# First eight microseconds of a residual-fusion kernel: one weight split moved to VectorE, tile 1 gathered in three parts and transposed between the first products

## The chip, the cores and the metric

The kernel runs on one core of a Trainium2 chip. The metric is the device time of one execution in microseconds (us), less is better. Three runs of the kernel before gave 101.44, 101.99 and 107.20 us; the median is 101.99 us.

## The reference

`x` has 4 rows of 1024 x 512, `cond` is 4 x 256, `W` is 1536 x 512, `b` has 512 numbers, all in 32-bit floats.

```python
hidden = concatenate([cond, cond], axis=-1)                  # 4 x 512
x_mean = mean(x, axis=1, keepdims=True)
fused  = concatenate([x, x_mean * ones, hidden * ones], -1)  # 4 x 1024 x 1536
return x + relu(einsum('bld,do->blo', fused, W) + b)
```

The first third of `W` multiplies `x` itself (4096 x 512 by 512 x 512, nearly all of the arithmetic). The second third multiplies the row's mean and the last third the condition; both, with `b`, are one bias vector for each of the 4 rows, which is added before the relu.

## The kernel before

The 4096 lines of `x` are 32 tiles of 128 x 512. For a product on TensorE a tile has to be transposed in four chunks of 128 columns, `j` from 0 to 3. For accuracy each operand is split into a high part in the reduced type `F32R` and a low part, which is what the high part leaves over, and a tile's result is the sum of 12 matrix products: for each chunk high x high (`n` = 0), low x high (`n` = 1) and high x low of `W` (`n` = 2). So there are 384 products of 128 x 512, on five PSUM banks `ps_o` (`po` in the profile); two more banks `ps_x` (`px`) and one `acc` take transposed chunks.

Every instruction stands in a table `ORDER`, written out by hand (lines 22 to 50). An engine runs its own instructions in that order and waits for what each of them reads, or for a buffer to be free. A name in the table is a task, and `@d`, `@a`, `@p` put it on VectorE (DVE), ScalarE (ACT) or GpSimd (POOL):

- `W0` to `W3` and `X0.0` to `X0.3` load the four chunks of `W`'s first third and the tiles 0 to 3; `Z4.1` and the like load later tiles in a layout that VectorE transposes.
- `y1.0` gathers part 0 of tile 1 (line 239 on DVE and POOL, 237 on ACT): it copies columns so that TensorE can transpose a chunk. `Y_PARTS` tells how many chunks a part has.
- `T1.0` transposes chunk 0 of tile 1 on TensorE (line 259) into a bank; the line above it says which.
- `h1.0` makes the high part on ACT (line 268, two instructions, the second reads the column sums), `l1.0` the low part on DVE (line 274).
- `wh1` makes the high part of chunk 1 of `W` (lines 218 and 220), `wl1` its low part (line 224). `wh0l` and `wh0r` are the left and right half of 256 columns.
- `p0.2.1` is the product of tile 0, chunk 2, `n` = 1 (line 365). A `fill` (line 134) is a product of zeros that keeps TensorE at work until data are there.

The tiles 0 to 3 go this way, one after the other; from tile 4 on, VectorE does the transposes. At the start the first tile's products are held up by what they need, chunk by chunk: the four chunks of `W` come in at some distance, `wl1` and `wl2` are made by POOL, `wh2` and `wh3` by ACT, and ACT also makes every `h`. In the table before, tile 1's two parts are gathered by `y1.0@d` and `y1.1@a`, its four transposes stand together behind `p0.0.1` and go to `acc`, `ps_o[3]`, `ps_x[0]` and `ps_x[1]`, and chunk 0 of `W` gets its low part from POOL.

Of the kernel before, what the change touches and what calls it, by code (L numbers as in the profile page):

```python
# [20 lines left out]

ORDER = """
W0@a fill X0.0 X0.1 W1 fill relu fill W2 fill X0.2 fill W3 fill X0.3 Z4.1 y0.0@d y0.1@a y0.2@p fill T0.0 T0.1 h0.0
T0.2 T0.3 fill wh0r@d h0.1 wh0l@d p0.0.0 wl0r@p l0.0@d h0.2 wl0l@p y1.0@d y1.1@a p0.0.1 h0.3 l0.1@d T1.0 T1.1 T1.2
T1.3 wh1@d h1.0 p0.0.2 l1.0@d h1.1 p0.1.0 p1.0.0 Z4.2 h1.2 p0.1.1 l0.2@d l0.3@d wl1@p p1.0.2 l1.1@d h1.3 p1.0.1 Z4.3
p1.1.0 wh2@a l1.2@d p1.1.1 y2.0@d p0.2.0 wl2@p l1.3@d T2.0 T2.1 T2.2 T2.3 p1.2.0 Z4.0 p0.2.1 h2.0 h2.1 h2.2 h2.3
l2.0@d l2.1@d wh3@a C p1.2.1 p0.1.2 p1.1.2 l2.2@d l2.3@d wl3@d p2.0.0 p2.0.1 p0.2.2 V p0.3.0 B p1.3.0 y3.0@d p0.3.1
p1.3.1 T3.0 T3.1 T3.2 T3.3 p1.2.2 p0.3.2 h3.0 h3.1 p1.3.2 l3.0@d h3.2 l3.1@d p2.0.2 h3.3 l3.2@d l3.3@d p2.1 p2.2 p2.3
p3.0 p3.1 Z5.0 Z5.2 Z5.3 p3.2 Z5.1 T4.0 T4.3 h4.0 T4.1 h4.3 l4.0@d h4.1 l4.3@p t3 p3.3 T4.2 M1 K2@d l4.1@p M0 K1@a
p4.0 t2 M2 h4.2 ac0@p p6.0 M3 l4.2@d K0@a p4.3 Z6.2 t0 K3@d p5.3 t1 Z6.3 ac1@d g0.0 p7.2 p6.2 d0.0 Z6.0 g0.1 p5.2 d0.1  # L30
g1.0 p5.0 Z6.1 T5.1 T5.3 p5.1 d1.0 T5.2 p6.3 K5@a Z7.0 T5.0 as0 p4.2 to0 g1.1 p7.3 Z7.3 h5.1 m0.0 p6.1 g2.0 l5.1@p
m0.1 p4.1 Z7.2 h5.2 m0.2 p7.1 K4@a m0.3 h5.3 p7.0 Z7.1 K6@a p8.1 l5.3@p l5.2@d h5.0 X4.1 p10.1 f0 Z8.2 d1.1 p9.1 fa0
Z8.1 p10.3 l5.0@d vh0 d2.0 p8.2 g2.1 vl0 Z8.0 p11.2 K7@a T6.3 d2.1 p11.3 T6.2 h6.3 Z8.3 p8.0 T6.0 l6.3@p T6.1 pb0
p10.0 bc0@a h6.0 p10.2 b1@p h6.1 X1.1 l6.0@d p9.3 X2.0 h6.2 b2@d p9.0 as1 Z9.2 to1 p9.2 r1@a l6.1@p l6.2@d p12.3 r2@a
X1.0 m1.0 K9@a p8.3 Z9.0 F1@p T7.3 p11.0 T7.1 h7.3 p12.2 b0@p m1.1 h7.1 p12.0 T7.2 K8@a p12.1 b3@p g3.0 T7.0 p11.1
K10@a m1.2 Z10.3 h7.2 d3.0 p13.1 Z9.3 m1.3 h7.0 p14.0 Z9.1 l7.0@d f1 b4@p p13.3 r0@a l7.2@d p14.1 r3@a T8.2 l7.3@p
p15.0 fa1 Z10.2 p13.0 T8.0 vh1 F2@p p15.1 K11@a vl1 X5.0 p13.2 F0@d Z10.0 b6@p p15.2 S1 T8.3 pb1 X5.1 l7.1@p p14.3
bc1@a as2 p14.2 K13 F3@p r6@a p16.0 K12 h8.3 p15.3 K14 h8.2 l8.3@p T8.1 p17.0 b5@d h8.1 p19.3 b9@p h8.0 p17.3 r4@a
l8.0@d p19.2 to2 g3.1 l8.2@d F4@p p16.2 r5@a m2.0 p18.3 K15 b8@p S4 p18.2 Z10.1 m2.1 p16.3 X3.1 d3.1 m2.2 p19.0 m2.3
p18.1 F5@p T9.0 p16.1 f2 fa2 p20.3 b11@p S5 T9.3 S2 p17.2 vh2 X3.0 h9.0 vl2 p17.1 F6@p X2.1 h9.3 S3 T9.2 p19.1 l8.1@d  # L40
b7@p S6 p20.0 X4.0 pb2 S0 p18.0 bc2@a l9.3@p X7.0 h9.2 p20.2 K17 r7@a p20.1 K16 as3 F7@p p22.2 T9.1 l9.0@d p21.3 h9.1
T10.0 S7 r8@a p21.1 l9.1@p X6.1 K19 r11@a p22.1 r9@a l9.2@d b10@p p22.0 r14@a K18 p21.2 r13@a T10.1 h10.0 p24.2 F13@p
T10.2 h10.1 p24.1 T10.3 h10.2 F8@p F9@d p21.0 r15@a p24.0 r10@a F11@p S8 K20 h10.3 p22.3 S13 K21 r17@a p23.1 X6.0 to3
r21@a p23.0 F10@p m3.0 r18@a p23.3 r20@a m3.1 p26.1 l10.3@p m3.2 p25.0 K22 F21@p p23.2 m3.3 r22@a p26.2 F15@p f3 S21
p24.3 S11 r12@a fa3 p27.3 S10 F17@p K23 S15 vh3 p25.1 S9 r16@a vl3 p25.2 r19@a F16@p r23@a p26.0 l10.0@d p25.3 F19@p
S16 pb3 X7.1 p26.3 bc3@a S17 F12@p P28 p27.1 K25 p27.2 l10.2@d P30 F18@p p28.2 F14@d r25@a p30.2 l10.1@p K26 p28.0 S14
S18 F25@d P31l p27.0 S19 F23@p r26@a p30.0 K24 S25 p31.2l F26@p S23 K27 p31.0l r24@a S12 p31.1l P29 p31.3l F20@p p30.3
P31r F31l F22@d S31l p29.1 S26 p28.1 S20 r27@d S22 p29.0 F24@d F27@p p28.3 p29.3 F28 S24 p30.1 S27 S28 p29.2 F30
p31.1r F29 S30 p31.0r p31.3r S29 p31.2r F31r S31r
""".split()  # L50


# [1 line left out]
def kernel(  # L54
# [9 lines left out]
    B, L, D = x.shape  # L64
# [9 lines left out]
    E = 4  # L74
    UNITS = [(0, 1), (1, 1), (2, 1), (3, 1)] + [(t, 4) for t in range(4, NT, 4)]
    BY_PE = (0, 1, 2, 3)
    Y_PARTS = {0: [(0, 1), (1, 1), (2, 2)], 1: [(0, 2), (2, 2)]}
    X_SLOT = [2, 3, 4, 5, 0, 1, 2, 3]
    X_PARTS = {0: [(0, 1), (1, 1), (2, 1), (3, 1)]}
    W_SLOT, COND_SLOT = 0, 1  # L80
# [34 lines left out]
    ps_o = [banks.tile([P, D], F32, name=f"po{i}") for i in range(O_BANKS)]  # L115
    ps_x = [banks.tile([P, D], F32, name=f"px{i}") for i in range(2)]
    acc = banks.tile([P, D], F32, name="acc")
# [23 lines left out]
    def task(name):  # L141
        def put(f):
            assert name not in tasks, name
            tasks[name] = f
        return put
# [17 lines left out]
    def z_of(u):  # L163
        return (u - len(BY_PE)) % Z_BUFS

    @task("relu")
    def _(e):
        nc.scalar.activation(one, one, AF.Relu)
# [58 lines left out]
    def gathered(t):  # L227
        return parks[PARKS - 1 - t]

    for t in range(sum(UNITS[u][1] for u in BY_PE)):  # L230
        for h, (j0, n) in enumerate(Y_PARTS.get(t, [(0, J)])):
            @task(f"y{t}.{h}")
# [8 lines left out]
    for u, (t0, n) in enumerate(UNITS):  # L241
        r = t0 // NK
        s = row_units[r].index(u)
        for j in range(J):
            buf, col = place[u, j]
            m = n * P
            if u == 0:
                xT = ((ps_x[0], ps_x[1], ps_o[4], ps_o[4])[j])[:, j % 2 * m : (j % 2 + 1) * m]
            elif u in BY_PE:
                xT = (ps_o[4] if u == 3 and j == 1 else (acc, ps_o[3], ps_x[0], ps_x[1])[j])[:, :m]  # L250
            else:
                xT = (turned if j % 2 else ps_x)[j // 2]

            @task(f"T{u}.{j}")
            def _(e, u=u, j=j, t0=t0, n=n, xT=xT):
                if u in BY_PE:
                    for i in range(n):
                        v = gathered(t0 + i)[:, j * P : (j + 1) * P]
                        nc.tensor.transpose(xT[:, i * P : (i + 1) * P], v, ident)  # L259
                    return  # L260
                nc.vector.transpose(  # L261
                    xT.rearrange("p (n q e) -> p n q e", q=Q // E, e=E),
                    zs[z_of(u)][:, : n * NQ].rearrange("p n (q j e) -> p n j q e", j=J, e=E)[:, :, j],
                )

            @task(f"h{u}.{j}")
            def _(e, r=r, j=j, s=s, xT=xT, buf=buf, col=col, m=m):
                nc.scalar.activation(  # L268
                    his[buf][:, col : col + m], xT, AF.Copy, accum_out=sums[:, r, j, s : s + 1]
                )  # L270

            @task(f"l{u}.{j}")
            def _(e, xT=xT, buf=buf, col=col, m=m):
                nc_of[e].tensor_tensor(  # L274
                    los[buf][:, col : col + m], xT, his[buf][:, col : col + m].bitcast(F32), ALU.subtract
                )
# [114 lines left out]
    for t in range(NT):  # L391
        r, k = divmod(t, NK)
        if t == LAST:
            for h in range(2):
                d = slice(h * HALF, (h + 1) * HALF)
# [93 lines left out]
```

## Time and profile before

| | us |
|---|---|
| median of the 3 runs | 101.99 |
| lowest and highest run | 101.44, 107.20 |
| the profiled execution | 101.22 |
| its span, from the first instruction to the last | 99.4 |
| TensorE (PE) busy in the span | 94.5 |
| GpSimd (POOL) busy | 79.6 |
| VectorE (DVE) busy | 77.5 |
| ScalarE (ACT) busy | 61.6 |

The profile is of one execution of its own, whose time was 101.22 us: 1.8 us lie around the span. Moments in the rows count from the span's start. A matmul overlaps the next one, so that its own duration is longer than its share of the time; the chain of waits gives each only what it adds.

### The profile page before, as it was taken

Reading aid. Unit: us, or ns where it says so; the run is one execution under the profiler, and the core shown is the slowest. Engines: PE = TensorE matmul, PEld = TensorE weight load, DVE = VectorE, ACT = ScalarE, POOL = GpSimd, SP = SyncE. Lnnn points to the kernel's source line nnn. Section 1 sums busy time; section 2 is a strip of 40 time slices with the busy share of each in tenths; the row PEclk is TensorE's granted clock in tenths of the full one; section 3 lists DMA queues with packets and bytes.
Section 4 is the critical chain, followed back from the end, with each engine's and each line's share of the span. In section 5 each row is a group of like instructions: output and inputs, shape, how many; then the busy total and the mean of one; then the engine's idle time right before and its main releaser. Section 6 shows DMA issues by size and latency. Waiting matters only on the chain.

```text
span 99.4 us, 1448 instructions
## 1 busy us (share of the span) xinstructions
PE 94.5 (95%) x424; PEld 76.4 (77%) x424; DVE 77.5 (78%) x132; ACT 61.6 (62%) x160; POOL 79.6 (80%) x77
## 2 busy tenths in 40 slices
PE   6999999999999999999999999999999999999940
PEld 2468888888888888888888888888888887888830
DVE  1396559959498979989699899899769769969930
ACT  4495338555996699994299227499973897350000
POOL 5287002969869989999999999999999999999600
PEclk9999999999999999999999999999999999999999
DMA  2999999999999999999999999999998369998894
GB/s 49 343 346 283 213 301 287 204 263 330 198 209 209 222 250 216 234 345 241 219 215 226 246 374 291 381 297 407 407 391 263 115 255 304 331 382 329 303 381 151
DMA packets 25361, 27.36 MB, mean 275 GB/s; under 512 B 1413, under 2 KB 16009, under 8 KB 25354
## 3 DMA queue, kind: packets, MB, share of 16 engines
q1 hardware_dynamic: 25210, 27.01, 101.0%
q10 hardware_dynamic: 144, 0.26, 0.8%
q8 instruction: 3, 0.05, 0.2%
q14 instruction: 4, 0.03, 0.1%
HBM read 18.88 MB, written 8.39 MB: 274 GB/s over the span
## 4 chain that ended last, share of the span: by engine, by line
PE 95%; DVE 1%; issue 0%
PE po L365 88%; PE po L134 4%; PE px L259 1%; PE acc L343 1%; PE po L259 1%; PE acc L259 0%; DVE x L403 0%; DVE warm L125 0%; DVE one L126 0%
## 5 line engine op out<-in xcount | busy, mean ns | idle before, releaser
L365 PE MATMUL po<-w_hi,hi 128*128 128x512 f32 (+1 forms) x132 | 50.5, 385 | 0.0
L365 PE MATMUL po<-w_hi,lo 128*128 128x512 f32 (+1 forms) x132 | 50.3, 384 | 0.0
L365 PE MATMUL po<-w_lo,hi 128*128 128x512 f32 (+1 forms) x132 | 50.1, 384 | 0.0
L454 POOL TENSOR_TENSOR x<-o,x 128x512 f32<-128x512 f32 x22 | 29.8, 1377 | 0.4 <-DVE o L445 0.4
L365 PEld LDWEIGHTS po<-w_hi,hi 128*128 128x128 f32 x132 | 24.8, 188 | 5.1 <-ACT hi L268 0.3
L365 PEld LDWEIGHTS po<-w_hi,lo 128*128 128x128 f32 x132 | 24.8, 188 | 5.1 <-DVE lo L274 0.2
L365 PEld LDWEIGHTS po<-w_lo,hi 128*128 128x128 f32 x132 | 24.7, 188 | 4.9 <-POOL w_lo L224 0.2
L274 POOL TENSOR_TENSOR lo<-xT,hi 128x512 fp32r<-128x512 f32 x13 | 17.3, 1333 | 8.6 <-ACT hi L268 8.5
L447 ACT ACTIVATE o<-o 128x512 f32<-128x512 f32 x27 | 15.7, 621 | 3.4 <-DVE o L440 3.0
L436 POOL TENSOR_TENSOR o<-o,bias 128x512 f32<-128x512 f32 x10 | 14.3, 1431 | 0.0
L319 DVE SCALAR_TENSOR_TENSOR acc<-w_mean,tot,acc 128x512 f32<-128x512 f32 x16 | 12.0, 748 | 2.6 <-POOL tot L310 2.3
L440 DVE TENSOR_TENSOR o<-po,bias 128x512 f32<-128x512 f32 x16 | 10.5, 684 | 3.6 <-ACT bias L347 2.1
L274 DVE TENSOR_TENSOR lo<-px,hi 128x512 fp32r<-128x512 f32 (+1 forms) x22 | 11.6, 537 | 1.1 <-ACT hi L268 1.0
L268 ACT ACTIVATE hi<-px 128x512 fp32r<-128x512 f32 (+1 forms) x22 | 10.4, 477 | 2.9 <-DVE px L261 2.3
L261 DVE STREAM_TRANSPOSE xT<-z 128x512 f32<-128x512 f32 x14 | 9.4, 688 | 1.3 <-DMA z<-in_x_dram 1.2
L261 DVE STREAM_TRANSPOSE px<-z 128x512 f32<-128x512 f32 x14 | 9.5, 699 | 1.1 <-DMA z<-in_x_dram 1.0
L268 ACT ACTIVATE hi<-xT 128x512 fp32r<-128x512 f32 x14 | 8.7, 624 | 0.8 <-DVE xT L261 0.6
L296 ACT ACTIVATE term<-wc,cT 128x512 f32<-128x512 f32 x8 | 5.7, 716 | 2.3 <-DVE cT L282 1.6
L454 DVE TENSOR_TENSOR x<-o,x 128x512 f32<-128x512 f32 x6 | 6.5, 1081 | 0.0
L432 ACT ACTIVATE o<-po 128x512 f32<-128x512 f32 x10 | 5.9, 587 | 0.7 <-PE po L365 0.7
L300 POOL TENSOR_TENSOR cond<-b_sb,term 128x512 f32<-128x512 f32 x4 | 5.2, 1295 | 1.0 <-ACT term L296 1.0
L300 POOL TENSOR_TENSOR cond<-cond,term 128x512 f32<-128x512 f32 x4 | 5.2, 1300 | 0.2
(61 smaller groups left out, 72.5 us busy)
## 6 DMA issues: line engine op xcount, KB each, us to landing
out_dram<-x SPq DMA_DIRECT2D x31, 256.0 KB, 3.2
z<-in_x_dram SPq DMA_DIRECT2D x28, 256.0 KB, 8.6
x<-in_x_dram SPq DMA_DIRECT2D x14, 512.0 KB, 8.1
x<-in_x_dram SPq DMA_DIRECT2D x4, 256.0 KB, 4.0
x<-in_L_cond_W_dram SPq DMA_DIRECT2D x1, 1024.0 KB, 8.2
w_mean<-in_L_cond_W_dram SPq DMA_DIRECT2D x4, 256.0 KB, 7.5
x<-in_L_cond_W_dram SPq DMA_DIRECT2D x3, 256.0 KB, 4.1
x<-in_L_cond_W_dram ACTq DMA_DIRECT2D x1, 256.0 KB, 3.7
```

The source lines that it names most:

```text
L261: nc.vector.transpose(xT.rearrange("p (n q e) -> p n q e", q=Q // E, e=E), zs[z_of(u)][:, : n * NQ].rearrange("p n (q j e) -> p n j q e", ...
L268: nc.scalar.activation(his[buf][:, col : col + m], xT, AF.Copy, accum_out=sums[:, r, j, s : s + 1])
L274: nc_of[e].tensor_tensor(los[buf][:, col : col + m], xT, his[buf][:, col : col + m].bitcast(F32), ALU.subtract)
L296: nc.scalar.activation(terms[k], wc[:, k], AF.Copy, scale=cT[:, k, r : r + 1])
L300: nc.gpsimd.tensor_tensor(conds[r % 2], conds[r % 2] if k else b_sb, terms[k], ALU.add)
L319: nc.vector.scalar_tensor_tensor(acc, w_mean[:, j, :], tot[:, r, j : j + 1], acc, ALU.mult, ALU.add)
L365: nc.tensor.matmul(v, lhsT=a[:, col : col + P], rhs=m, start=WAYS[t] != "I" and key not in done, stop=done.count(key) == 3 * J - 1, skip_g ...
L432: nc.scalar.activation(o, bank(t), AF.Copy)
L436: nc_of[e].tensor_tensor(o, o, biases[r], ALU.add)
L440: nc.vector.tensor_tensor(o, bank(t), biases[r], ALU.add)
L447: nc.scalar.activation(o, o, AF.Relu)
L454: nc_of[e].tensor_tensor(x_tile(t), o, x_tile(t), ALU.add)
```

## The change

Chunk 0 of `W` gets its low part on VectorE, in two halves behind `l0.0`. Tile 1 is gathered in three parts, the first two of one chunk each by ACT, the third of two chunks by VectorE. Its transposes are split up: `T1.0` and `T1.1` stay where the four stood, `T1.2` and `T1.3` come seven products later, and the banks for the tiles 1 to 3 are named one by one. The products of the tiles 0 and 1 are put in another order up to the transposes of tile 2. GpSimd loses two instructions and VectorE gets one more, since its gather of tile 1 takes the place of another. The order of the DMAs on SyncE is the same as before.

```diff
-T0.2 T0.3 fill wh0r@d h0.1 wh0l@d p0.0.0 wl0r@p l0.0@d h0.2 wl0l@p y1.0@d y1.1@a p0.0.1 h0.3 l0.1@d T1.0 T1.1 T1.2
-T1.3 wh1@d h1.0 p0.0.2 l1.0@d h1.1 p0.1.0 p1.0.0 Z4.2 h1.2 p0.1.1 l0.2@d l0.3@d wl1@p p1.0.2 l1.1@d h1.3 p1.0.1 Z4.3
+T0.2 T0.3 fill wh0r@d h0.1 wh0l@d p0.0.0 l0.0@d y1.0@a wl0r@d p0.0.1 y1.1@a wl0l@d T1.0 h0.2 T1.1 p0.0.2 h1.0 wh1@d
+h0.3 p1.0.0 l0.1@d wl1@p p0.1.0 h1.1 l1.0@d p1.0.2 y1.2@d p1.0.1 wh2@a Z4.2 p0.1.1 l1.1@d p1.1.0 l0.2@d p0.2.0 T1.2
...
-    Y_PARTS = {0: [(0, 1), (1, 1), (2, 2)], 1: [(0, 2), (2, 2)]}
+    Y_PARTS = {0: [(0, 1), (1, 1), (2, 2)], 1: [(0, 1), (1, 1), (2, 2)]}
...
             elif u in BY_PE:
-                xT = (ps_o[4] if u == 3 and j == 1 else (acc, ps_o[3], ps_x[0], ps_x[1])[j])[:, :m]
+                two = {1: (ps_o[3], ps_o[2], ps_x[0]), 2: (ps_o[3], ps_x[0], ps_x[1]), 3: (ps_o[4], ps_x[0], ps_x[1])}
+                xT = (acc, *two[u])[j][:, :m]
```

On VectorE, from the low part of tile 0's chunk 0 on, the kernel before had these rows (`o_113` is the gathered tile 1, `lo_89` and `lo_90` belong to the tiles 0 and 1, `w_hi<-x_63` is a high part of `W`):

```order
L274 TENSOR_TENSOR lo_89<-px_141,hi_75 128x128
L239 COPY o_113<-x_65 128x256
L274 TENSOR_TENSOR lo_89<-px_142,hi_75 128x128
L220 CAST w_hi<-x_63 128x512
L274 TENSOR_TENSOR lo_90<-acc,hi_76 128x128
L274 TENSOR_TENSOR lo_89<-po_140,hi_75 128x128 x2
```

Now the same place reads:

```order
L275 TENSOR_TENSOR lo_89<-px_141,hi_75 128x128
L224 TENSOR_TENSOR w_lo<-x_63,w_hi 128x256 x2
L220 CAST w_hi<-x_63 128x512
L275 TENSOR_TENSOR lo_89<-px_142,hi_75 128x128
L275 TENSOR_TENSOR lo_90<-acc,hi_76 128x128
L239 COPY o_113<-x_65 128x256
L275 TENSOR_TENSOR lo_90<-po_139,hi_76 128x128
L275 TENSOR_TENSOR lo_89<-po_140,hi_75 128x128 x2
```

The two halves of chunk 0's low part stand in front of `wh1`, and the gather on this engine has moved behind `l1.0`; it is now of the chunks 2 and 3.

On TensorE, from `p0.0.1` on, the kernel before had (`po_136` and `po_137` are the results of the tiles 0 and 1):

```order
L365 MATMUL po_136<-w_hi,lo_89 128x512
L259 MATMUL acc<-term_123,o_113 128x128
L259 MATMUL po_139<-term_123,o_113 128x128
L259 MATMUL px_141<-term_123,o_113 128x128
L259 MATMUL px_142<-term_123,o_113 128x128
L365 MATMUL po_136<-w_lo,hi_75 128x512
L365 MATMUL po_136<-w_hi,hi_75 128x512
L365 MATMUL po_137<-w_hi,hi_76 128x512
```

Now:

```order
L366 MATMUL po_136<-w_hi,lo_89 128x512
L260 MATMUL acc<-term_123,o_113 128x128
L260 MATMUL po_139<-term_123,o_113 128x128
L366 MATMUL po_136<-w_lo,hi_75 128x512
L366 MATMUL po_137<-w_hi,hi_76 128x512
L366 MATMUL po_136<-w_hi,hi_75 128x512
L366 MATMUL po_137<-w_lo,hi_76 128x512
```

Two of tile 1's four transposes are gone from here, and `p1.0.0` stands one place ahead of `p0.1.0`.

Further on, around the transposes of tile 2 (`o_112`), TensorE had before, from `T2.1` to `p0.3.0`:

```order
L259 MATMUL po_139<-term_123,o_112 128x128
L259 MATMUL px_141<-term_123,o_112 128x128
L259 MATMUL px_142<-term_123,o_112 128x128
L365 MATMUL po_137<-w_hi,hi_76 128x512
L365 MATMUL po_136<-w_hi,lo_89 128x512
L365 MATMUL po_137<-w_hi,lo_90 128x512
L365 MATMUL po_136<-w_lo,hi_75 128x512
L365 MATMUL po_137<-w_lo,hi_76 128x512
L365 MATMUL po_138<-w_hi,hi_77 128x512
L365 MATMUL po_138<-w_hi,lo_91 128x512
L365 MATMUL po_136<-w_lo,hi_75 128x512
L365 MATMUL po_136<-w_hi,hi_75 128x512
```

Now:

```order
L260 MATMUL po_139<-term_123,o_112 128x128
L260 MATMUL px_141<-term_123,o_112 128x128
L260 MATMUL px_142<-term_123,o_112 128x128
L366 MATMUL po_137<-w_hi,lo_90 128x512
L366 MATMUL po_138<-w_hi,hi_77 128x512
L366 MATMUL po_138<-w_hi,lo_91 128x512
L366 MATMUL po_136<-w_lo,hi_75 128x512
L366 MATMUL po_136<-w_hi,hi_75 128x512
```

Four of the five products that stood between `T2.3` and `p2.0.0` (`po_138`) now stand ahead of `T2.0`; one is left. From `p2.0.0` on, TensorE's order is the one of before to the end, and so is that of the other engines from `h2.0`, `l2.0` and `wl2` on.

## Rows read from the trace of the kernel before

**Rows 1.** The page, part 2: TensorE's granted clock in 40 slices, in tenths

```profile
PEclk9999999999999999999999999999999999999999
```

**Rows 2.** Chain that ended last, by time: start us, us added, engine, tile, line

```profile
5.34 0.47 PE po L365 x2
5.80 0.24 PE acc L259
6.04 0.11 PE po L259
...
6.37 2.33 PE po L365 x9
8.70 0.11 PE acc L259
...
9.13 2.76 PE po L365 x12
11.90 0.11 PE acc L259
...
12.33 22.02 PE po L365 x97
...
95.52 0.42 DVE x L403
```

**Rows 3.** Windows: stretch, engines' busy us (instructions), granted clock, DMA share, GB/s

```profile
12.33:95.50 83.17, 83.16 (x378) 68.90 (x376) 70.32 (x107) 54.65 (x129) 73.62 (x64) 1.00 1.05 281
```

**Rows 4.** Who waited for whom, TensorE's weight loads: us in total, times, longest

```profile
PEld acc L259 <- DVE o L239: 0.5, 2, 0.3
...
PEld po L365 <- POOL w_lo L224: 0.2, 1, 0.2
```

**Rows 5.** Timeline of TensorE: start us, us, engine, line, operation [idle before <-releaser]

```profile
0.97 3.17 PE L134 MATMUL po<-warm 128*128 128x512 bf16 x7 [0.97 <-DVE one L126]
...
6.30 0.51 PE L365 MATMUL po<-w_lo,hi 128*128 128x512 f32 x1
```

**Rows 6.** Timeline of DVE, 5 to 12 us: y1.0, wh1, y2.0, wl3, y3.0

```profile
5.02 0.64 DVE L239 COPY o<-x 128x256 f32<-128x256 f32 x1
...
5.79 0.73 DVE L220 CAST w_hi<-x 128x512 fp32r<-128x512 f32 x1
...
7.48 0.72 DVE L239 COPY o<-x 128x512 f32<-128x512 f32 x1
...
10.54 0.69 DVE L224 TENSOR_TENSOR w_lo<-x,w_hi 128x512 fp32r<-128x512 f32 x1 [0.23 <-ACT w_hi L218]
11.15 0.42 DVE L239 COPY o<-x 128x512 f32<-128x512 f32 x1
```

**Rows 7.** Timeline of ACT, 3 to 11 us: y0.1, h0.1, y1.1, wh2, h2.0, wh3

```profile
3.55 0.31 ACT L237 ACTIVATE o<-x 128x128 f32<-128x128 f32 x1 [0.70 <-DMA x<-in_x_dram]
...
4.67 0.27 ACT L268 ACTIVATE hi<-px 128x128 fp32r<-128x128 f32 x1
...
5.32 0.41 ACT L237 ACTIVATE o<-x 128x256 f32<-128x256 f32 x1
...
7.09 0.65 ACT L218 ACTIVATE w_hi<-x 128x512 fp32r<-128x512 f32 x1
8.85 0.28 ACT L268 ACTIVATE hi<-acc 128x128 fp32r<-128x128 f32 x1 [1.10 <-PE acc L259]
...
9.86 0.65 ACT L218 ACTIVATE w_hi<-x 128x512 fp32r<-128x512 f32 x1
```

**Rows 8.** Timeline of POOL: both halves of wl0, first half alone, wl1, wl2

```profile
4.78 1.46 POOL L224 TENSOR_TENSOR w_lo<-x,w_hi 128x256 fp32r<-128x256 f32 x2 [0.75 <-DVE w_hi L220]
...
4.78 0.73 POOL L224 TENSOR_TENSOR w_lo<-x,w_hi 128x256 fp32r<-128x256 f32 x1 [0.75 <-DVE w_hi L220]
...
6.61 1.30 POOL L224 TENSOR_TENSOR w_lo<-x,w_hi 128x512 fp32r<-128x512 f32 x1 [0.37 <-DVE w_hi L220]
...
7.87 1.47 POOL L224 TENSOR_TENSOR w_lo<-x,w_hi 128x512 fp32r<-128x512 f32 x1
```

More of the change, by code (lines that the diff above doesn't have):

```diff
@@ L23 @@
 W0@a fill X0.0 X0.1 W1 fill relu fill W2 fill X0.2 fill W3 fill X0.3 Z4.1 y0.0@d y0.1@a y0.2@p fill T0.0 T0.1 h0.0
-T0.2 T0.3 fill wh0r@d h0.1 wh0l@d p0.0.0 wl0r@p l0.0@d h0.2 wl0l@p y1.0@d y1.1@a p0.0.1 h0.3 l0.1@d T1.0 T1.1 T1.2
-T1.3 wh1@d h1.0 p0.0.2 l1.0@d h1.1 p0.1.0 p1.0.0 Z4.2 h1.2 p0.1.1 l0.2@d l0.3@d wl1@p p1.0.2 l1.1@d h1.3 p1.0.1 Z4.3
-p1.1.0 wh2@a l1.2@d p1.1.1 y2.0@d p0.2.0 wl2@p l1.3@d T2.0 T2.1 T2.2 T2.3 p1.2.0 Z4.0 p0.2.1 h2.0 h2.1 h2.2 h2.3
-l2.0@d l2.1@d wh3@a C p1.2.1 p0.1.2 p1.1.2 l2.2@d l2.3@d wl3@d p2.0.0 p2.0.1 p0.2.2 V p0.3.0 B p1.3.0 y3.0@d p0.3.1
@@ L28 @@
[L28 to L47, printed above, removed]
@@ L48 @@
-P31r F31l F22@d S31l p29.1 S26 p28.1 S20 r27@d S22 p29.0 F24@d F27@p p28.3 p29.3 F28 S24 p30.1 S27 S28 p29.2 F30
-p31.1r F29 S30 p31.0r p31.3r S29 p31.2r F31r S31r
+T0.2 T0.3 fill wh0r@d h0.1 wh0l@d p0.0.0 l0.0@d y1.0@a wl0r@d p0.0.1 y1.1@a wl0l@d T1.0 h0.2 T1.1 p0.0.2 h1.0 wh1@d
+h0.3 p1.0.0 l0.1@d wl1@p p0.1.0 h1.1 l1.0@d p1.0.2 y1.2@d p1.0.1 wh2@a Z4.2 p0.1.1 l1.1@d p1.1.0 l0.2@d p0.2.0 T1.2
+T1.3 l0.3@d p1.1.1 h1.2 Z4.3 h1.3 wl2@p y2.0@d p0.1.2 p1.1.2 l1.2@d p0.2.1 l1.3@d p1.2.0 T2.0 T2.1 T2.2 T2.3 p1.2.1
@@ new lines @@
+Z4.0 h2.0 h2.1 h2.2 h2.3 l2.0@d l2.1@d wh3@a C l2.2@d l2.3@d wl3@d p2.0.0 p2.0.1 p0.2.2 V p0.3.0 B p1.3.0 y3.0@d
+p0.3.1 p1.3.1 T3.0 T3.1 T3.2 T3.3 p1.2.2 p0.3.2 h3.0 h3.1 p1.3.2 l3.0@d h3.2 l3.1@d p2.0.2 h3.3 l3.2@d l3.3@d p2.1
+p2.2 p2.3 p3.0 p3.1 Z5.0 Z5.2 Z5.3 p3.2 Z5.1 T4.0 T4.3 h4.0 T4.1 h4.3 l4.0@d h4.1 l4.3@p t3 p3.3 T4.2 M1 K2@d l4.1@p
+M0 K1@a p4.0 t2 M2 h4.2 ac0@p p6.0 M3 l4.2@d K0@a p4.3 Z6.2 t0 K3@d p5.3 t1 Z6.3 ac1@d g0.0 p7.2 p6.2 d0.0 Z6.0 g0.1
+p5.2 d0.1 g1.0 p5.0 Z6.1 T5.1 T5.3 p5.1 d1.0 T5.2 p6.3 K5@a Z7.0 T5.0 as0 p4.2 to0 g1.1 p7.3 Z7.3 h5.1 m0.0 p6.1 g2.0
@@ new lines @@
+l5.1@p m0.1 p4.1 Z7.2 h5.2 m0.2 p7.1 K4@a m0.3 h5.3 p7.0 Z7.1 K6@a p8.1 l5.3@p l5.2@d h5.0 X4.1 p10.1 f0 Z8.2 d1.1
+p9.1 fa0 Z8.1 p10.3 l5.0@d vh0 d2.0 p8.2 g2.1 vl0 Z8.0 p11.2 K7@a T6.3 d2.1 p11.3 T6.2 h6.3 Z8.3 p8.0 T6.0 l6.3@p T6.1
+pb0 p10.0 bc0@a h6.0 p10.2 b1@p h6.1 X1.1 l6.0@d p9.3 X2.0 h6.2 b2@d p9.0 as1 Z9.2 to1 p9.2 r1@a l6.1@p l6.2@d p12.3
+r2@a X1.0 m1.0 K9@a p8.3 Z9.0 F1@p T7.3 p11.0 T7.1 h7.3 p12.2 b0@p m1.1 h7.1 p12.0 T7.2 K8@a p12.1 b3@p g3.0 T7.0
+p11.1 K10@a m1.2 Z10.3 h7.2 d3.0 p13.1 Z9.3 m1.3 h7.0 p14.0 Z9.1 l7.0@d f1 b4@p p13.3 r0@a l7.2@d p14.1 r3@a T8.2
@@ new lines @@
+l7.3@p p15.0 fa1 Z10.2 p13.0 T8.0 vh1 F2@p p15.1 K11@a vl1 X5.0 p13.2 F0@d Z10.0 b6@p p15.2 S1 T8.3 pb1 X5.1 l7.1@p
+p14.3 bc1@a as2 p14.2 K13 F3@p r6@a p16.0 K12 h8.3 p15.3 K14 h8.2 l8.3@p T8.1 p17.0 b5@d h8.1 p19.3 b9@p h8.0 p17.3
+r4@a l8.0@d p19.2 to2 g3.1 l8.2@d F4@p p16.2 r5@a m2.0 p18.3 K15 b8@p S4 p18.2 Z10.1 m2.1 p16.3 X3.1 d3.1 m2.2 p19.0
+m2.3 p18.1 F5@p T9.0 p16.1 f2 fa2 p20.3 b11@p S5 T9.3 S2 p17.2 vh2 X3.0 h9.0 vl2 p17.1 F6@p X2.1 h9.3 S3 T9.2 p19.1
+l8.1@d b7@p S6 p20.0 X4.0 pb2 S0 p18.0 bc2@a l9.3@p X7.0 h9.2 p20.2 K17 r7@a p20.1 K16 as3 F7@p p22.2 T9.1 l9.0@d
@@ new lines @@
+p21.3 h9.1 T10.0 S7 r8@a p21.1 l9.1@p X6.1 K19 r11@a p22.1 r9@a l9.2@d b10@p p22.0 r14@a K18 p21.2 r13@a T10.1 h10.0
+p24.2 F13@p T10.2 h10.1 p24.1 T10.3 h10.2 F8@p F9@d p21.0 r15@a p24.0 r10@a F11@p S8 K20 h10.3 p22.3 S13 K21 r17@a
+p23.1 X6.0 to3 r21@a p23.0 F10@p m3.0 r18@a p23.3 r20@a m3.1 p26.1 l10.3@p m3.2 p25.0 K22 F21@p p23.2 m3.3 r22@a p26.2
+F15@p f3 S21 p24.3 S11 r12@a fa3 p27.3 S10 F17@p K23 S15 vh3 p25.1 S9 r16@a vl3 p25.2 r19@a F16@p r23@a p26.0 l10.0@d
+p25.3 F19@p S16 pb3 X7.1 p26.3 bc3@a S17 F12@p P28 p27.1 K25 p27.2 l10.2@d P30 F18@p p28.2 F14@d r25@a p30.2 l10.1@p
@@ L50 @@
+K26 p28.0 S14 S18 F25@d P31l p27.0 S19 F23@p r26@a p30.0 K24 S25 p31.2l F26@p S23 K27 p31.0l r24@a S12 p31.1l P29
+p31.3l F20@p p30.3 P31r F31l F22@d S31l p29.1 S26 p28.1 S20 r27@d S22 p29.0 F24@d F27@p p28.3 p29.3 F28 S24 p30.1 S27
+S28 p29.2 F30 p31.1r F29 S30 p31.0r p31.3r S29 p31.2r F31r S31r
 """.split()
```

## The prediction

> **What bounds the kernel now.** I read the chain of waits first, since it tells which engine sets the end. From 5.34 us to the last product it is TensorE alone, and only VectorE's last 0.42 us and a store follow [rows 2]. Behind tile 3's transposes 97 products add 22.02 us, 0.227 each [rows 2], and from 12.33 to 95.50 TensorE is busy for 83.16 of 83.17 us [rows 3]. So TensorE never waits there: what it loses or gains before 12.33 arrives at the end in full, as long as no other engine becomes late.
>
> Then I looked for time lost before 12.33. The measure is a product at 0.23 and a transpose at 0.11. Where `T1.0` adds 0.24 in place of 0.11, 0.13 are lost. The nine products behind tile 1's transposes add 2.33 in place of 2.07: 0.26 lost. The twelve behind tile 2's add 2.76, 0.23 each: nothing lost [rows 2]. The waits agree in place: a transpose waited for a gather on VectorE, a product for a low part of `W` from POOL [rows 4]. So the most that a better order of the start can save is 0.39 us, 0.4% of the time. (About 2% is what a measurement of this kernel can tell from no change.)
>
> How close the next place is to waiting is the point. `T2.0` ends at 8.81. ACT begins `h2.0` at 8.85, makes four high parts in 1.01 and begins `wh3` at 9.86, for 0.65 [rows 7]. `wl3` starts 0.03 behind that, `y3.0` 0.61 later for 0.42, to 11.57 [rows 6]. From the end of a gather to the end of the transpose that needs it took 0.38: `y1.0` ended at 5.66, `T1.0` at 6.04 [rows 2, 6]. From `T2.0`'s end to `T3.0`'s this chain over ACT and VectorE takes 0.04 + 1.01 + 0.65 + 0.03 + 0.61 + 0.42 + 0.38 = 3.14. The measured distance is 8.81 to 12.01, 3.20 [rows 2]. It hid with 0.06 to spare, under three transposes, twelve products and `T3.0`: 0.33 + 2.76 + 0.11 = 3.20.
>
> **The change, part by part.** *Low part of chunk 0.* POOL's two instructions took 4.78 to 6.24 [rows 8], and `p0.0.2` ended at 6.81 [rows 5], 0.57 behind them. On VectorE two of 256 columns start at 5.02, where `y1.0` stood [rows 6]. No row shows that size with two operands in SBUF; 512 columns took 0.69 with POOL idle [rows 6]. The two together cost between 0.69 and, with the start of a second instruction, 0.90; I take 0.76, nearer the row. They end at 5.78 and `p0.0.2` at 6.35.
>
> *Gather and transposes of tile 1.* ACT takes `y1.0` behind `h0.1`, which began at 4.67; a high part with its sums takes 0.25, a quarter of the 1.01 above. So 4.95 + 0.31, the time of `y0.1`, makes 5.26 [rows 7]. `y1.1` ends by 5.57. `p0.0.1` still ends at 5.80, so `T1.0` and `T1.1` end at 5.91 and 6.02, not held up: the 0.13 are saved. Then `p0.0.2` would be due at 6.25 and comes at 6.35, 0.10 lost. `p1.0.0` needs `h1.0`, which starts 0.04 behind `T1.0`, takes 0.28 and ends at 6.23 (before, four transposes and another product gave it more room); with 0.57 the product ends at 6.80, not at 6.58: 0.22 lost. `p0.1.0` needs `wh1`: 5.79, when chunk 1 had landed, and 0.42 as `y3.0` with POOL idle, 6.21 [rows 6]; not late, it ends at 7.03. Lost here 0.32, before 0.39: the start gains 0.07.
>
> *Up to tile 2.* Ten products and three transposes follow: 7.03 + 2.30 + 0.33 puts `T2.0`'s end at 9.66. What they need is earlier: `wh2` by ACT behind `h1.1` from about 6.75; `wl1` on POOL from 6.30 to 7.60, before a product that ends at 8.87; `wl2` to about 9.05, before one due past 11. `T1.2` and `T1.3` go to banks that are free by then.
>
> *From tile 2 to tile 3.* Four products that covered ACT's chain are now spent ahead of `T2.0`. Under the chain are left 0.33 + 8 x 0.23 + 0.11 = 2.28, and the chain is as long as before, since none of its instructions changes: `T3.0` ends at 9.66 + 3.14 = 12.80, before 12.01. TensorE stands idle for 0.86 there, a little in front of `p2.0.0` and `p2.0.1` (they need `h2.0` and `l2.0`), most of it in front of `p0.3.0`, which needs `wh3`, and the rest in front of `T3.0`; its queue is in order, so all products behind them wait too. This is the whole cost: 0.86 lost, 0.07 gained, **0.79 us later**. Behind `T3.0` the order is the same and nothing in it was short, so the 0.79 stay to the end. The moved loads cost nothing: SyncE's order is the same.
>
> *Two copies of VectorE beside POOL.* Three of its copies beside POOL's splits end just behind them: `y1.0` at 5.66, POOL's first half at 5.51; `wh1` at 6.52, POOL's second half at 6.24; `y2.0` at 8.20, `wl1` at 7.91 [rows 6, 8]. `y3.0`, alone, took 0.42. These rows can be read as copies that wait until POOL's instruction ends, or as copies that run slower. Now `y1.2` comes at 6.55 and `y2.0` at about 8.3, both into POOL's splits. Slower by as much as before, they end at 7.2 and 9.0, and `T2.0` is at 9.66. Waiting, `y1.2` ends at 7.75, `wl2` at 9.05, `y2.0` at 9.33, and `T2.0` at 9.33 + 0.38 = 9.71; the sum is then 0.84. The Trainium skill, "SBUF — State Buffer", section "SBUF: two separate sides", states the first reading as a rule: VectorE and GpSimd share a pair of ports under an exclusive lock for a whole instruction, and the other fully blocks. By that rule the trace's three ends agree with a block, and the change gathers tile 2 as late as TensorE wants it.
>
> The sum is made against the profiled execution: 101.22 + 0.79 = 102.0 (span 99.4 to 100.2). The median of the runs shown is 0.77 above that execution. Which of the two stands nearer to another set of runs can't be told from three; I take the middle, 101.6, and forecast 102.4.
>
> **The rivals.** *The cover still holds.* Something on ACT's chain starts earlier than its rows say, TensorE doesn't stand in front of `p0.3.0`, and the start's gain is what is left: -0.07, 101.5 from the middle; at most the whole 0.39, 101.2. For it: every step before 7 us gets shorter or leaves POOL. Against: the chain is of the same instructions on one engine after another and had 0.06 to spare. This is faster, but within 2%.
>
> *More is late than that.* Chunk 2 had landed by 7.09, when ACT began `wh2` [rows 7]; if no sooner, `p0.2.0` ends at 7.74 + 0.57 = 8.31 in place of 8.18, 0.13 more. With the block beside POOL and a `wl0` at its upper bound the cost is 1.0 to 1.2, 102.6 to 102.8. For it: early loads come in close to their use. Against: between chunk 1, used at 5.79, and 7.09 lies more than a microsecond.
>
> *TensorE falls to its lower clock.* The gap between the tiles 2 and 3 is longer than any since its start. The seven fills at the start add 3.17, 0.45 each, where a product of the same 512 columns later takes 0.23 [rows 2, 5]: that is 1.2 and 2.4 GHz, though the granted clock reads full throughout [rows 1]. If the level fell, each product would cost 0.20 more, and from seven such products on (0.79 + 1.40 = 2.19) the change is slower by over 2%, at least 103.8. Against: after 0.39 lost in 2 us the pace stayed at 0.23. The Trainium skill, "TensorE: Matmul & The Clock Gate", section "HAM oscillation — how this bites in real kernels", tells of kernels that fall to the half rate in waits for data; no run here shows that.
>
> **How the numbers follow.** The forecast, 0.4 to 1.0 later, gets 0.69: its chain is measured link by link. The cover that holds, in whole or in part, gets 0.20; more lateness, up to under 2%, 0.07; the lower clock 0.03. 0.01 is left for a gain over 2%, which no row supports. The first three lie within 2%: faster 0.01, same 0.96, slower 0.03. The range goes from 101.2, the profiled execution with the start's gain or the middle with all of it, to 103.5: the median with 0.79 is 102.8, with the late chunk and the block 103.0, and 0.5 is for runs that differ among themselves by 0.77.
>
> **What would show it.** Right: two low parts of 256 columns on VectorE from 5.02, mean 0.35 to 0.45; POOL idle to 6.3; `T2.0` ends near 9.7; TensorE's weight loads wait some 0.5 for ACT's `wh3` (a row that before lacks), and a little for `y3.0`; `T3.0` ends near 12.8; no waits behind. Wrong in size: `wh3` begins well before 10.6, or `T3.0` ends by 12.3. Wrong in kind: products at 0.43 after 12 us, or new gaps past tile 4.

## The result and the profile after

The changed kernel took 102.57 us (median of 18 runs), the kernel before, beside it, 102.09. The ratio is 1.0067, with a 95% interval of 1.0039 to 1.0095: 0.4 to 1.0 us slower, 0.7 at the middle. The forecast was 102.4 us and 0.8 us slower. (Ratios leave out slow runs.) Two counts of the change differ from what was said above: eight products stand between `T1.1` and `T1.2`, and VectorE has two instructions more than before, 134 for 132, ScalarE one more.

The page of the changed kernel, parts 1 and 2, as in [rows 1]:

```profile
PE 95.6 (95%) x424; PEld 76.7 (76%) x424; DVE 78.5 (78%) x134; ACT 61.7 (61%) x161; POOL 77.9 (77%) x75
...
PEclk9999999999999999999999999999999999999999
```

Its chain of waits, to set beside [rows 2] (start us, us added, engine, tile, line):

```profile
4.99 0.43 PE po L134
5.42 0.85 PE po L366 x2
6.27 0.16 PE acc L260
6.43 0.02 issue
6.45 0.38 ACT hi L269 x2
6.83 0.04 issue
6.87 1.89 PE po L366 x7
...
10.14 0.12 PE acc L260
10.27 0.02 issue
10.29 0.24 ACT hi L269
10.53 0.03 issue
10.56 0.87 ACT hi L269 x6
11.43 0.53 ACT w_hi L218
11.96 0.04 issue
12.00 1.20 PE po L366 x4
13.20 0.20 PE acc L260
...
13.72 22.03 PE po L366 x97
...
96.93 0.42 DVE x L404
```

Before, this chain was TensorE's from 5.34 on. Now ACT stands in it twice: at 6.45, where `p1.0.0` waits for `h1.0`, and from 10.29 to 11.96, where the four high parts of tile 2 and then `wh3` are waited for. `T2.0` ends at 10.26, `T3.0` at 13.40, 3.14 later. Behind tile 3's transposes 97 products add 22.03, as before 22.02. The waits of TensorE's weight loads from 5 us on say the same as sums (us in total, times, longest); the first row had no counterpart before, while the wait for POOL's `w_lo` of [rows 4] is gone:

```profile
PEld po L366 <- ACT w_hi L218: 0.7, 1, 0.7
PEld po L366 <- ACT hi L269: 0.6, 2, 0.4
PEld acc L260 <- DVE o L239: 0.3, 1, 0.3
```

The profiled execution took 102.6 us, 1.38 more than that of before, twice the 0.7 by which the runs differ. Part of it is not the change: the first two products add 0.85 us here, 0.47 before. Another execution of the same kernel had them at 0.47 too (the run `g2` below).

### The profile page after: what moved, and what is told of

It is laid out like the page before. It is cut to its first block, busy times and chain, and to the rows that moved or that the text cites. A ratio compares the mean times of both kernels' runs of the same rounds, so it can differ in the third digit from the quotient of the medians.

```text
span 100.8 us, 1450 instructions
## 1 busy us (share of the span) xinstructions
PE 95.6 (95%) x424; PEld 76.7 (76%) x424; DVE 78.5 (78%) x134; ACT 61.7 (61%) x161; POOL 77.9 (77%) x75
## 4 chain that ended last, share of the span: by engine, by line
PE 93%; ACT 2%; DVE 1%; issue 0%
PE po L366 87%; PE po L134 4%; ACT hi L269 1%; PE acc L344 1%; PE px L260 1%; PE po L260 1%; ACT w_hi L218 1%; PE acc L260 0%; DVE x L404 0%; DVE warm L125 0%; DVE one L126 0%
## 5 line engine op out<-in xcount | busy, mean ns | idle before, releaser
L366 PE MATMUL po<-w_hi,lo 128*128 128x512 f32 (+1 forms) x132 | 50.9, 388 | 0.0
```

What stands on the lines that cost most here:

```text
L366: nc.tensor.matmul(v, lhsT=a[:, col : col + P], rhs=m, start=WAYS[t] != "I" and key not in done, stop=done.count(key) == 3 * J - 1, skip_g ...
```

## The experiments

Landmarks of every profile, from the timelines of TensorE (start plus duration of the instruction, us). "Rest" is the time from `T3.3`'s end to the last product's. Sums of rounded rows in the text can be 0.01 or 0.02 off the table.

| run | `p0.0.0` ends | `T2.0` ends | `T3.0` ends | `T2.0` to `T3.0` | rest | ratio to before, 95% interval |
|---|---|---|---|---|---|---|
| before | 5.57 | 8.81 | 12.01 | 3.20 | 83.15 | |
| the change | 5.85 | 10.25 | 13.40 | 3.15 | 83.17 | 1.0067, 1.0039 to 1.0095 |
| e1, products ahead | 5.85 | 9.99 | 13.13 | 3.14 | 83.10 | 1.0065, 1.0025 to 1.0105 |
| e2, wh3 early | 5.85 | 10.32 | 12.87 | 2.54 | 86.84 | 1.0029, 0.9985 to 1.0072 |
| e3, and p2.0 late | 5.47 | 9.61 | 12.04 | 2.42 | 84.01 | 0.9983, 0.9942 to 1.0025 |
| e4, wl0 alone | 5.43 | 8.77 | 11.96 | 3.20 | 83.16 | 0.9996, 0.9932 to 1.0060 |
| f1, the change | 5.84 | 10.32 | 13.46 | 3.15 | 85.33 | 0.9853, 0.9784 to 0.9923 |
| f2, one more ahead | 5.86 | 10.73 | 13.88 | 3.14 | 83.15 | 0.9918, 0.9864 to 0.9973 |
| f3, tile 1 first | 5.36 | 9.46 | 11.93 | 2.47 | 83.47 | 0.9808, 0.9734 to 0.9883 |
| g1, tile 1 first | 5.61 | 9.89 | 12.36 | 2.47 | 84.14 | 1.0031, 0.9993 to 1.0069 |
| g2, the change | 5.63 | 9.80 | 12.94 | 3.14 | 83.26 | 1.0023, 0.9989 to 1.0056 |

The three f runs stood beside a kernel before that took 103.18 us or more in all of its 11 runs there; its fastest run in the other sets lay at 100.87 to 101.35. The changed kernel took there what it took elsewhere (fastest run 102.15, in the first set 101.79). So those three ratios lie below 1 because the kernel before was slower in that set. Why it was is not known, and they are not read as gains of a schedule; but it isn't shown either that the loss is the same wherever the kernel runs.

**e1: only the four products ahead of tile 2's transposes, in the kernel before.**

```diff
-p0.2.0 wl2@p l1.3@d T2.0 T2.1 T2.2 T2.3 p1.2.0 Z4.0 p0.2.1 h2.0 ... C p1.2.1 p0.1.2 p1.1.2 l2.2@d
+p0.2.0 wl2@p l1.3@d p1.2.0 p0.2.1 p0.1.2 p1.1.2 T2.0 T2.1 T2.2 T2.3 Z4.0 h2.0 ... C p1.2.1 l2.2@d
```

> The kernel before with one thing of the change alone: four products (p1.2.0, p0.2.1, p0.1.2, p1.1.2) stand ahead of T2.0 in place of behind T2.3. Theory (the cover of ACT's chain is spent): T2.0 ends 0.92 us later than before, the distance from T2.0's end to T3.0's stays at 3.1 to 3.2 us, TensorE's weight loads wait 0.5 to 0.7 us for wh3, and the time is 0.8 to 0.9 us above before, ratio about 1.008. Rival (what the change costs comes from its first part, from TensorE's later rise to the higher clock or from VectorE's longer queue): the distance shrinks to about 2.3 us, no wait for wh3, time as before within 0.2 us.

The chain of waits of this run:

```profile
9.88 0.12 PE acc L259
10.01 0.02 issue
10.03 1.14 ACT hi L268 x8
11.17 0.53 ACT w_hi L218
11.70 0.04 issue
11.74 1.19 PE po L365 x4
12.93 0.20 PE acc L259
```

This is the same chain over ACT as in the changed kernel, of the same length, with nothing else of the change in it; `wh3` is waited for by 0.7 us (weight loads, from 5 to 14 us). `T2.0` ended 1.18 later than before, not 0.92, since here too the first products went at the slower pace. The ratio, 1.0065, is the changed kernel's: the order of these four products alone makes a loss of that size. With 0.4% to each side, the ratios do not exclude that the other parts of the change add or take a few tenths of a microsecond.

**e2: the change, with `wh3` and `wl3` where ACT and VectorE had stood idle.**

```diff
-Z4.0 h2.0 h2.1 h2.2 h2.3 l2.0@d l2.1@d wh3@a C l2.2@d l2.3@d wl3@d p2.0.0
+Z4.0 wh3@a wl3@d h2.0 h2.1 h2.2 h2.3 l2.0@d l2.1@d C l2.2@d l2.3@d p2.0.0
```

> The changed kernel with wh3 on ACT ahead of h2.0 and wl3 on VectorE ahead of l2.0, where both engines stood idle for 0.75 us and more; nothing else moves. Theory (ACT's chain is the cost): no wait for wh3 is left; TensorE still waits some 0.3 us for l2.0 in front of p2.0.1; T2.0's end to T3.0's is 2.5 to 2.7 us in place of 3.14, the time 0.4 to 0.6 us below the changed kernel, ratio to before 0.999 to 1.003. Rival (the cost sits in front of T2.0): the distance shrinks all the same, but a wait elsewhere takes its place and the ratio stays at 1.006 to 1.008.

The timeline of TensorE, `T2.0` and `T3.0`:

```profile
10.05 0.27 PE L260 MATMUL acc<-term,o 128*128 128x128 f32 x1
...
12.60 0.27 PE L260 MATMUL acc<-term,o 128*128 128x128 f32 x1
```

2.54 lie between them in place of 3.15, and no wait for `wh3` is left, as expected. The middle of the ratio, 1.0029, moved as expected too, but its interval reaches to the changed kernel's. The profiled execution took 105.77 us with waits behind 49 us, so only its first 13 us are read.

**e3: e2, with `p2.0.0` and `p2.0.1` behind `p1.3.1`.**

```diff
-l2.2@d l2.3@d p2.0.0 p2.0.1 p0.2.2 V p0.3.0 B p1.3.0 y3.0@d
-p0.3.1 p1.3.1 T3.0
+l2.2@d l2.3@d p0.2.2 V p0.3.0 B p1.3.0 y3.0@d
+p0.3.1 p1.3.1 p2.0.0 p2.0.1 T3.0
```

> The run before this one with p2.0.0 and p2.0.1 behind p1.3.1 as well, so that h2.0 and l2.0 have four products more to be made in. Theory: TensorE has no wait from T2.0 to T3.0, the distance is 2.3 us, and the start's gain is what is left: the time 0.0 to 0.2 us below before, ratio 0.998 to 1.000, some 0.8 us below the changed kernel. Rival: the same as in the run before, ratio 1.006 to 1.008; or T3.0 now waits for y3.0, which comes behind l2.3, and 0.1 to 0.3 us are left.

`T3.0` ends at 12.04, as early as before (12.01) with all of the change's start in it, 2.42 behind `T2.0`. The ratio's middle lies 0.9 us below the changed kernel's, and the two intervals do not meet. The ratio is in the expected range, but its interval holds 1, so a gain on before isn't shown. In the profile the rest is 84.01 in place of 83.15. New waits stand at tile 4, in the timelines of VectorE and of TensorE's weight loads (first before, then e3):

```profile
14.55 0.73 DVE L261 STREAM_TRANSPOSE px<-z 128x512 f32<-128x512 f32 x1 [1.04 <-DMA z<-in_x_dram]
```

```profile
15.66 0.73 DVE L262 STREAM_TRANSPOSE px<-z 128x512 f32<-128x512 f32 x1 [2.12 <-DMA z<-in_x_dram]
```

```profile
18.18 0.19 PEld L366 LDWEIGHTS po<-w_hi,lo 128*128 128x128 f32 x1 [0.32 <-DVE lo L275]
...
18.87 0.19 PEld L366 LDWEIGHTS po<-w_hi,hi 128*128 128x128 f32 x1 [0.39 <-ACT o L433]
```

VectorE waits 2.12 us for the load of tile 4 and starts its transposes at 15.66; in the profile of before it started them at 14.55. The order of the loads is the same: this execution's loads landed later. That doesn't go by the start: f2, whose `T3.0` ended at 13.88, also started them at 15.66, and its TensorE did not wait there. Further on the chain of waits of e3 passes through POOL, and TensorE goes on only when a low part is done there:

```profile
82.62 4.24 POOL x L455 x3
86.86 1.71 POOL lo L275
88.62 7.77 PE po L366 x41
```

So in this execution TensorE is not the only bound: loads and POOL are close behind it. The start is not shorter here than before, so it isn't a shorter start that brings them up. In e4, whose `T3.0` ended at 11.96 and whose tile 4 had landed by 14.45, the rest was 83.16:

```profile
14.45 0.73 DVE L261 STREAM_TRANSPOSE px<-z 128x512 f32<-128x512 f32 x1 [0.99 <-DMA z<-in_x_dram]
```

**e4: only chunk 0's low part moved, behind `y1.0`, in the kernel before.**

```diff
-wh0l@d p0.0.0 wl0r@p l0.0@d h0.2 wl0l@p y1.0@d y1.1@a
+wh0l@d p0.0.0 l0.0@d h0.2 y1.0@d wl0r@d wl0l@d y1.1@a
```

> The kernel before with the low part of W's chunk 0 on VectorE alone, behind y1.0; tile 1 is gathered in two parts and transposed in one piece as before, and the products keep their order. Theory: y1.0 and wh1, with POOL idle, take about 0.30 and 0.42 us in place of 0.64 and 0.73; T1.0 and p0.0.2 come 0.1 to 0.2 us earlier, the cover behind tile 2 stays, and the time is 0.1 to 0.2 us below before, ratio 0.998 to 0.999. Rival (a longer queue on VectorE delays wh1 and the low parts): p0.1.0 waits, ratio 1.000 to 1.003.

The timeline of VectorE, `y1.0`, both halves of `wl0`, and `wh1`:

```profile
4.99 0.29 DVE L239 COPY o<-x 128x256 f32<-128x256 f32 x1
5.20 0.75 DVE L224 TENSOR_TENSOR w_lo<-x,w_hi 128x256 fp32r<-128x256 f32 x2
...
6.07 0.42 DVE L220 CAST w_hi<-x 128x512 fp32r<-128x512 f32 x1
```

The durations are the expected ones: with POOL idle, 0.29 for 0.64 and 0.42 for 0.73 [rows 6]. `T1.0` ended at 5.77, not 6.04, yet `p0.0.2` at 6.77 and `T2.0` at 8.77, each 0.04 earlier than before and not 0.1 to 0.2: a transpose now waited 0.5 us for VectorE (`l0.1`, behind the two new instructions, frees the bank). So the rival's longer queue on VectorE is real, though it held up a transpose and not `p0.1.0`. The ratio, 0.9996 with an interval of 1.3%, can't tell a gain of 0.1 us from none.

**f1 and g2: the changed kernel again, unaltered.**

> The changed kernel unaltered, for a second profile of it. In its first profile TensorE's first two products went at the lower pace (0.43 us each) until 6.27 us, as they also did in the run with only four products moved, whose start is that of before. Theory (when TensorE rises to the higher level belongs to the execution, not to the change; the change costs 0.8 us through the distance T2.0 to T3.0): this profile may show either level at p0.0.1; at the higher one T2.0 ends at 9.6 to 9.8 and T3.0 at 12.7 to 12.9, in both the distance is 3.1 to 3.2; ratio 1.004 to 1.010. Rival (the change delays the rise): the first two products stand at 0.43 again and T2.0 ends past 10.1.

> The changed kernel unaltered, on the same chip as the run before this one. Theory: ratio to before 1.004 to 1.010 where before runs at 101 to 102 us; T2.0's end to T3.0's 3.1 to 3.2 us; p0.0.1 at either pace. Rival (the change itself makes the kernel faster wherever the loads come late): ratio below 0.995 again.

f1's first products stood at 0.43 each again and `T2.0` ended at 10.32, as the rival of that run had it (the profiled execution took 104.67 us, with a wait of 2.4 us for VectorE at 55 us). In g2 they did not, and e1 shows the slower pace with the start of before: so the change isn't needed for it, nor does it always bring it. The chain of waits of g2:

```profile
5.39 0.47 PE po L366 x2
5.86 0.12 PE acc L260
5.98 0.02 issue
6.00 0.38 ACT hi L269 x2
6.38 0.04 issue
6.42 1.87 PE po L366 x7
...
9.69 0.12 PE acc L260
...
11.54 1.20 PE po L366 x4
12.74 0.20 PE acc L260
```

This is the execution to set beside before, since both have the higher pace from `p0.0.1` on: `T2.0` ends at 9.81, `T3.0` at 12.94, 0.93 later than before. Its ratio was 1.0023, below the 1.004 to 1.010 that was expected, and its interval holds 1. It may be that where the loads come later, some of the loss meets waits that would have come anyway; that is a guess from e3, and no run shows it. The rival, a ratio below 0.995, did not come true, but the kernel before ran at its usual time here, so that what was different in the set of f1 was not met again. The intervals of the first set and of this one overlap from 1.0039 to 1.0056, 0.4 to 0.6 us.

**f2: one more product, `p1.2.1`, ahead of `T2.0`.**

```diff
-p1.2.0 T2.0 T2.1 T2.2 T2.3 p1.2.1
+p1.2.0 p1.2.1 T2.0 T2.1 T2.2 T2.3
```

> The changed kernel with the last covering product, p1.2.1, ahead of T2.0 too, so that p2.0.0 follows T2.3 at once. Theory (the distance T2.0 to T3.0 is ACT's and VectorE's chain, whatever TensorE has to do in it): the distance stays at 3.1 to 3.2 us with seven products in it in place of eight, T2.0 ends 0.23 us later or a little more, the time is 0.2 to 0.3 us above the changed kernel, ratio to before about 1.009. Rival (the distance follows the number of products): it shrinks by 0.23 and the time is the changed kernel's.

The distance stays at 3.14 with seven products in it; `T3.0` ends at 13.88, 0.42 behind f1's, whose first products went at the same pace. So the distance follows the chain and not the number of products. The delay is larger than the 0.23 of the product, since the product waited for `l1.2`:

```profile
10.12 0.19 PEld L366 LDWEIGHTS po<-w_hi,lo 128*128 128x128 f32 x1 [0.36 <-DVE lo L275]
```

It ended at 10.63 and not at 10.42.

**f3 and g1: e3, with `T1.0` and `T1.1` ahead of `p0.0.1`.**

```diff
-wl0r@d p0.0.1 y1.1@a wl0l@d T1.0 h0.2 T1.1 p0.0.2
+wl0r@d y1.1@a wl0l@d T1.0 h0.2 T1.1 p0.0.1 p0.0.2
```

> The run with wh3 early and p2.0.0, p2.0.1 late, and T1.0, T1.1 one place earlier, ahead of p0.0.1, so that h1.0 starts 0.2 us sooner. Theory (what the start still loses is the wait of p1.0.0 for h1.0): p1.0.0 comes without a wait, p0.1.0 ends 0.2 us earlier counted from p0.0.0, T2.0 to T3.0 stays at 2.4 us, the time is 0.2 to 0.4 us below before, ratio 0.996 to 0.998. Rival (from tile 4 on the loads of z set the pace, so that a start that is shorter than that of before only waits there): the start is as short, but TensorE waits behind tile 4's first parts by as much, ratio 0.999 to 1.002.

> The run with wh3 early, p2.0.0 and p2.0.1 late and T1.0, T1.1 ahead of p0.0.1, unaltered, beside other runs of the kernel before: those of the last call lay at 103.2 us and more, so that a ratio to them says nothing on the schedule. Theory (both waits of the start are gone): 0.2 to 0.4 us below before where before runs at 101 to 102 us, ratio 0.996 to 0.998, and 0.9 to 1.2 us below the changed kernel of the same call. Rival (the loads of z take over): ratio 0.999 to 1.002.

In f3 `p1.0.0` came without its wait, and `T3.0` ended at 11.93, the earliest of all. But from `p0.0.0`'s end `p0.1.0` came only 0.1 earlier than in g2, not 0.2, and in g1 `p1.0.0` still waited 0.2 for `h1.0` and `p0.1.0` 0.2 for `wh1`. In f3 tile 1's last transposes now come as soon as their gather is done, and the waits of the weight loads from 7 to 13 us are VectorE's:

```profile
PEld acc L260 <- DVE o L239: 0.3, 1, 0.3
PEld po L260 <- DVE o L239: 0.2, 1, 0.2
PEld px L260 <- DVE lo L275: 0.2, 1, 0.2
```

`T3.0` ended 0.11 before e3's, but so had `p0.0.0` (5.36 and 5.47): what was gained in front of `p1.0.0` was lost again by tile 2. The ratio of g1 is 1.0031, no gain: the forecast of 0.996 to 0.998 missed. So did the other half of it, 0.9 to 1.2 us below the changed kernel of the same set: the medians were 102.17 for g1 and 102.12 for g2. In the profiles `T3.0` ended 0.58 earlier in g1 than in g2, but the rest was 0.88 longer, with waits of the weight loads for VectorE at 75 us (0.8) and for POOL at 89 us (0.4). Which of this is the execution and which the order isn't shown. Outside the set of the f runs no version beat the kernel before by more than the interval.

## Why the prediction was right

*What bounds it.* TensorE without waits behind tile 3: the rest is 83.15 before, 83.17 after, 83.26 in g2. For the change the step held in these profiles. It isn't a property of the kernel: in e3, f3 and g1, whose `T3.0` ended between 11.93 and 12.36, the rest grew by 0.3 to 1.0, while in e4 with 11.96 it did not. "Nothing in it was short" was read from one execution in which tile 4 had landed by 14.55; in most of the others it was 0.6 to 1.4 later. g1 shows what hangs on it: a start 0.58 shorter than g2's gave no shorter time.

*The start.* The prediction had a gain of 0.07: 0.39 lost before, 0.32 after, in front of `p0.0.2` and `p1.0.0`. In g2 `T2.0` ended at 9.81, not 9.66, and without the four products (0.92) that is 8.89 beside 8.81: nothing was gained. The term that was mis-sized is the wait of `p1.0.0` for `h1.0`: it was put at 0.22, with 0.10 for `p0.0.2` beside it. In g2 `p0.0.2` ended at 6.31, when it was due, and `p1.0.0` at 6.92 in place of 6.54: it alone lost 0.38, as much as the 0.39 that were lost before. In the chain it waits for both instructions of `h1.0`, 0.38 from 6.00 (the second reads the column sums), where the prediction counted the first alone, 0.28. The pair of low parts took 0.75 on VectorE, where 0.76 was forecast.

*From tile 2 to tile 3.* This is the step that carried the forecast, and it held. The chain was put at 3.14 and measured 3.14 to 3.15 in three profiles of the change, 3.14 in e1 and f2. Under it lay 2.28 of work, so the wait was 0.86, as forecast, and it stands where the prediction put it: in the first profile some 0.26 in front of `p2.0.0` and `p2.0.1`, 0.5 in front of `p0.3.0`, 0.09 in front of `T3.0`. e1 shows that this term alone gives a loss of the size measured, and e2 and e3 that the wait goes when `wh3` leaves the chain and the products of tile 2 leave their place. The rival "the cover still holds" is out.

*The size.* By the profiles the change costs 0.93 up to `T3.0` (g2) where 0.79 was forecast, and 0.06 of it stands at `p0.0.0` already. The runs gave 0.7 in the first set and 0.2 in that of g2. That the absolute time was met, 102.57 for 102.4, is in part luck: the base of 101.6 lay 0.5 below the 102.09 of the kernel before in the same set, and the difference of the two medians, 0.48, was smaller than the forecast one.

*More is late.* `wh2` began at 7.22 in the first profile and 6.77 in g2 and was not waited for: chunk 2 was there. *The lower clock.* Behind the gap of 0.7 us 97 products added 22.03, 0.227 each, so the level did not fall in these profiles.

*Copies beside POOL.* Timelines of VectorE and POOL in the changed kernel:

```profile
7.06 0.54 DVE L239 COPY o<-x 128x256 f32<-128x256 f32 x1
...
8.12 1.39 DVE L239 COPY o<-x 128x512 f32<-128x512 f32 x1
```

```profile
6.17 1.28 POOL L224 TENSOR_TENSOR w_lo<-x,w_hi 128x512 fp32r<-128x512 f32 x1 [2.19 <-DVE w_hi L220]
7.93 1.29 POOL L224 TENSOR_TENSOR w_lo<-x,w_hi 128x512 fp32r<-128x512 f32 x1 [0.48 <-ACT w_hi L218]
```

`y1.2` ended 0.15 behind `wl1` (7.60 and 7.45), `y2.0` 0.29 behind `wl2` (9.51 and 9.22), though it took 1.39 in place of 0.72. In g2 it took 0.91 and ended 0.29 behind `wl2` too (9.08 and 8.79); in e1, where `wl2` began only when the copy was nearly done, it took 0.41. A copy that only ran slower would not stretch with the time that POOL still needs; a copy that waits does. The Trainium skill, "SBUF — State Buffer", section "SBUF: two separate sides", has it so, an exclusive lock, and these rows agree. It had no price in the changed kernel: `T2.0` came after both.

## What to carry to other kernels

When products are moved ahead of something that starts a chain on another engine, count what is left under that chain: its length, from the transposes of one tile over ACT and VectorE to those of the next, was 3.14 us with seven products in it as with eight, and it had been covered with 0.06 us to spare. A stage that shows no wait in the profile may be the tightest one. And before a start is shortened by tenths, look at a second execution: what is next (here loads and POOL) may not show in the first.

## What the runs showed of the hardware that was not expected

The pace of TensorE's first products differs between executions, with the same start. `p0.0.0` and `p0.0.1` together added 0.47 us before and in g2, and 0.85 in the first profile of the change; the granted clock read full in all of them. These are the two levels of 2.4 and 1.2 GHz, by the 0.23 and 0.43 of a product. e1, whose instructions up to there are those of before, had 0.85 too. So it isn't the change, and a single profile can be off by 0.4 us for this alone. Of the eleven profiles five (the change, e1, e2, f1, f2) had `p0.0.0` end at 5.84 to 5.86, the others at 5.36 to 5.63.
